# A Golay-code filter and a two-expert layer on one core: bits turned by one product for four tiles, router pairs in four operations

## The chip, the cores and the metric

The kernel runs on one core of a Trainium2 chip. The metric is device time in microseconds (us), the median of several runs; lower is better. A further execution was recorded by the hardware profiler; its own time and span are given below. PE is TensorE, DVE is VectorE, ACT is ScalarE, POOL is GpSimd and SP is SyncE.

## The reference, cut to what matters

The input has 16384 tokens of 512 numbers. Each token is normalized, filtered along its 512 numbers by a circulant filter whose constants depend on the data, and projected to 24 bits. The bits are corrected by a code of 12 checks. The normalized token also goes to two of eight experts.

```
xn   = layernorm(x)                                # 16384 x 512
x1   = real(ifft(fft(xn) * filt))
bits = (sigmoid(x1 @ W_el + b_el) > 0.5)           # 24 per token
syn  = (bits @ H.T > 0.5)                          # 12 checks
w    = syn.sum(-1)
bits = where(0 < w <= 3, (bits + first three of syn) mod 2, bits)
s    = x1 + bits @ W_le + b_le
p    = softmax(xn @ router_w.T)                    # 8 experts
v, i = top_k(p, 2);  c = v / (v.sum + 1e-6)
g    = silu(sum over both of (xn @ expert[i] + v) * c)
out  = x + s * g
```

As w is at most 3 where a fix is made, the first three checks are all checks that failed, and the fix flips the bits 0 to 11 whose check failed.

## The kernel before, in words

Tokens lie in 128 tiles of 128 tokens, one token to a partition. Four tiles make a block (`TPT` = 4, one load of 1 MB), eight make a group (`GT` = 8), and sixteen a round (`RT` = 16). There are two passes, and in both the order of all instructions is written out by hand.

**The first pass** is `pass_1`, a loop over the tiles g. One turn of it issues, in this order: every fourth turn `take_ex` (L566, sums for a block its logits into `ex`), `fold` of tile g + 2, `level`, `total` and `spread` of tiles further ahead, `transpose` of tile g + 1 and `filt` of tile g. For one tile these are: `total` (DVE, L452: the two halves of a row added into pp, with the row's sum), `spread` (ACT, L472: a sum of squares), `fold` (DVE, L507 and L510, sums and differences of pp's halves; POOL, L512, the differences mm of the input's halves), `transpose` (PE, L519, four times; ACT, L521, copies pmt out), and `filt` (PE, L535, L536, L538; ACT, L541, writes yb). `store` (L551) sends a finished block of yb to the memory yd. `level` turns four row sums at a time into two numbers, by one ACT operation each: `low` (L465), minus four times the mean, which `fold` adds, and column 10 of the tile's record (L466), the mean, which the second pass reads.

After the tile's own work, one turn issues one operation of the list `now` and four of the list `routes`, and `throw(1)` issues one waiting scatter.

`now` holds, for each group, the five operations of `code`: `bits` (DVE, L577) compares 24 logits of eight tiles with a bound and writes them, 16 bits wide, into the record; `turn_bits(0)` and `turn_bits(4)` turn four tiles each so that the 24 bits lie on partitions (PE, L586, one product with the identity for each tile; ACT, L589, one copy of 24x512 out of PSUM); `syndrome` (PE, L596) multiplies the turned bits of each of the eight tiles by the 24x12 matrix `ht_b`; `correct` (DVE, L600 to L610) tests the checks and flips bits in the record.

`routes` holds, for each round, the operations of `route`, nearly all on DVE: a maximum and a softmax over eight logits, the two largest (`largest`, twice), `chosen` (L700, the sum of two one-hot rows, `sel`), `behind`, seven operations of `pair` (L726), `quads` (L740, sums over four tiles), an empty one, `rank` (PE, L748 to L772), `chances` (L665, L715 to L719: the two probabilities and the divisor), `weights` (L805 to L827: the two weights, the sum of the biases, and an exchange so that the smaller expert comes first), then `place` and `where` (positions in lists of the 28 pairs of experts), the sixteen scatters (POOL, L788, one indirect transfer each from `rec` to `lists`), `more` and an addition to `cum`, and `put_records` (SP, L627: the records go to yd in four transfers). `pair` for distance d multiplies `sel` of experts 0 to 7-d with that of experts d to 7; the 28 products of a token say which pair it chose.

The last group's `code` and the last round's `route` are issued in the second pass.

**The second pass** goes over tiles of one pair of experts each (`whole`, 28 at first and five later), over 61 tiles that straddle lists (`item`), and over a rest. For each tile POOL gathers the list's entry or addresses (`fetch_tok`), the tokens of x (xg, six tiles ahead) and of yd (yg, five ahead), all at L1154; `normalize` (DVE, L1208) subtracts the mean and multiplies; PE transposes (L1215) and multiplies by the experts (L1247); ACT and DVE combine (L1290 to L1298); `put` multiplies and adds (DVE, L1326) and sends the rows out (POOL, L1331), three tiles behind. In each turn it issues `throw(3)`, one operation of `now` and ten of `routes`, so the last round's operations are spread over the turns 0 to 5, and after them come operations that plan the later tiles (`whole_ops`, whose `kept` copies tokens, means and scales of the whole tiles).

Of the kernel before, what the change touches and what calls it, by code (L numbers as in the profile page):

```python
# [27 lines left out]
def pairs_of(ne=8):  # L28

    return [(a, a + d) for d in range(1, ne) for a in range(ne - d)]  # L30
# [3 lines left out]
def kernel(  # L34
# [114 lines left out]
    ht_b = p1c.tile([L, 12], BF16, name="ht_b")  # L149
# [39 lines left out]
    ht = sp.tile([L, 12], F32, name="ht")  # L189
# [253 lines left out]
    def total(g: int):  # L443

        k, j = groups[g // GT], g % GT
        if j == 0:
            k.sum = small.tile([P, GT], F32, name="sum")
            k.sq2 = small.tile([P, GT], F32, name="sq2")
            k.low = small.tile([P, GT], F32, name="low")
# [12 lines left out]
    def level():  # L462
        while means:
            k, js = means.pop()
            nc.scalar.activation(k.low[:, js], k.sum[:, js], AF.Copy, scale=-4.0 / E)  # L465
            nc.scalar.activation(k.rec[:, js, 10], k.sum[:, js], AF.Copy, scale=1.0 / E)  # L466
# [34 lines left out]
    def fold(g: int):  # L501
# [6 lines left out]
            sd[:, 0:Q], p[:, 0:Q], k.low[:, j : j + 1], p[:, Q:H], ALU.add, ALU.add  # L508
# [61 lines left out]
    def code(s: int):  # L570
# [3 lines left out]
        def bits():  # L574

            k.bits = bits_of(k.rec)[:, :, 0:L]
# [4 lines left out]
        def turn_bits(h):  # L581
            if h == 0:
                k.bt = small.tile([L, GT, P], BF16, name="bt", bufs=2)
            pg = ps_g.tile([P, 512], F32, name="pg")[0:L].rearrange("l (j t) -> l j t", t=P)
            for j in range(TPT):
                nc.tensor.matmul(  # L586
                    pg[:, j, :], k.bits[:, h + j, :], ident_b, start=True, stop=True
                )
            nc.scalar.copy(k.bt[:, h : h + TPT, :], pg)  # L589

        def syndrome():
            k.pg = ps_g.tile([P, 512], F32, name="pg")[:, 0 : GT * 12].rearrange(
                "p (j n) -> p j n", n=12
            )
            for j in range(GT):
                nc.tensor.matmul(k.pg[:, j, :], k.bt[:, j, :], ht_b, start=True, stop=True)  # L596

        def correct():
# [12 lines left out]
                k.bits[:, :, 0:12], k.bits[:, :, 0:12], fix, ALU.not_equal  # L611
# [20 lines left out]
    def route(n: int):  # L632
# [30 lines left out]
        def total():  # L663
            st.sm = new("sm", [P, S])
            v.tensor_reduce(st.sm, st.pb, AX.X, ALU.add)  # L665
# [32 lines left out]
        def chosen():  # L698
            st.sel = new("sel", SN, BF16)
            v.tensor_add(st.sel, st.hot1, st.hot2)  # L700
# [7 lines left out]
        def den_of():  # L708
            st.den = new("den", [P, S])
            v.tensor_add(st.den, st.sm, st.p2)  # L710

# [841 lines left out]
```

## Time and profile before

| | |
|---|---|
| median of 4 runs | 1467.51 us |
| lowest and highest run | 1463.81 and 1469.38 us |
| the profiled execution's own time | 1464.95 us |
| its span in the trace | 1463.2 us |
| mean TensorE clock granted in it | 0.969 of full |
| TensorE busy | 1338.8 us, 91% of the span |
| VectorE busy | 933.7 us, 64% |
| ScalarE busy | 603.7 us, 41% |
| GpSimd busy | 876.1 us, 60% |
| bytes moved by DMA | 234.27 MB |
| first pass, from the timeline | some 36 to 333 us |

Busy time counts the time in which an engine works on instructions; issuing of transfers and waiting for semaphores is not counted, and matmuls are pipelined with modelled ends. In a line of groups, `out<-in` are the names of the tiles, followed by partitions x elements and the count; then stand total busy time, the mean of one in ns, and the idle time just before them with what ended it.

### The profile page before, as it was taken

Reading aid. Unit: us, or ns where it says so; the run is one execution under the profiler, and the core shown is the slowest. Engines: PE = TensorE matmul, PEld = TensorE weight load, DVE = VectorE, ACT = ScalarE, POOL = GpSimd, SP = SyncE. Lnnn points to the kernel's source line nnn. Section 1 sums busy time; section 2 is a strip of 40 time slices with the busy share of each in tenths; the row PEclk is TensorE's granted clock in tenths of the full one; section 3 lists DMA queues with packets and bytes.
Section 4 is the critical chain, followed back from the end, with each engine's and each line's share of the span. In section 5 each row is a group of like instructions: output and inputs, shape, how many; then the busy total and the mean of one; then the engine's idle time right before and its main releaser. Section 6 shows DMA issues by size and latency. Waiting matters only on the chain.

```text
span 1463.2 us, 18162 instructions
## 1 busy us (share of the span) xinstructions
PE 1338.8 (91%) x4938; PEld 741.0 (51%) x4938; DVE 933.7 (64%) x2679; ACT 603.7 (41%) x1295; POOL 876.1 (60%) x855
## 2 busy tenths in 40 slices
PE   2999999997397999959999999999999999998996
PEld 2887777773143444424444444444444444444443
DVE  7798999972364588701111126768777787686784
ACT  4998999873221222202222222323333333232332
POOL 1357877676446454565555216777777777776741
PEclk9999999999698999989999999999999999999998
DMA  5799877735122332244444424555555555555531
GB/s 193 286 325 300 251 250 238 236 119 171 55 69 84 121 106 88 90 127 130 137 136 153 149 81 149 173 163 164 179 159 169 165 178 168 165 173 161 173 128 43
DMA packets 119215, 234.27 MB, mean 160 GB/s; under 512 B 37227, under 2 KB 70891, under 8 KB 115022
## 3 DMA queue, kind: packets, MB, share of 16 engines
q0 software_dynamic: 47264, 135.54, 30.5%
q1 hardware_dynamic: 70750, 96.81, 19.7%
q8 instruction: 43, 0.70, 0.2%
q10 hardware_dynamic: 1104, 0.78, 0.2%
q14 instruction: 54, 0.44, 0.1%
HBM read 145.31 MB, written 87.75 MB: 159 GB/s over the span
## 4 chain that ended last, share of the span: by engine, by line
PE 62%; issue 16%; POOL 10%; DVE 5%; ACT 3%; another core or an unknown queue 2%; DMA 2%; POOLq 0%; DVEq 0%; SPq 0%; ACTq 0%
PE pe L1247 40%; PE py L538 7%; PE pt L1215 4%; PE pt L519 3%; POOL out L1331 3%; POOL yg L1154 3%; POOL xg L1154 2%; PE py L535 2%; PE py L536 2%; POOL part L1154 1%; ACT no L472 1%; POOL entry L1154 1%; ACT yb L541 1%; PE pg L1280 1%
## 5 line engine op out<-in xcount | busy, mean ns | idle before, releaser
L1247 PE MATMUL pe<-w_sb,xt 128*128 x2104 | 949.1, 599 | 2.0 <-DVE acc L1297 1.5
L1247 PEld LDWEIGHTS pe<-w_sb,xt 128*128 128x128 f32 x2104 | 398.3, 192 | 425.0 <-issue 417.6
L1298 ACT ACTIVATE acc<-acc,yg 128x512 f32<-128x512 f32 x128 | 92.5, 722 | 420.4 <-DVE acc L1297 321.7
L1297 DVE SCALAR_TENSOR_TENSOR acc<-pe,yg,acc 128x512 f32<-128x512 f32 x101 | 75.7, 750 | 237.9 <-PE pe L1247 121.3
L1217 ACT COPY xt<-pt 128x512 f32<-128x512 f32 x162 | 93.9, 579 | 210.8 <-PE pt L1215 162.1
L1154 POOL DMA_INDIRECT yg<-yd,toks x101 | 111.4, 1103 | 114.8 <-ACT acc L1298 50.8
L1331 POOL DMA_INDIRECT out<-xg,toks x101 | 111.8, 1107 | 82.0 <-DVE xg L1326 55.5
L1208 DVE TENSOR_SCALAR xn<-xg,entry 128x512 f32<-128x512 f32 x61 | 33.6, 552 | 197.2 <-PE pt L1215 152.7
L512 POOL TENSOR_TENSOR mm<-xt 128x256 f32<-128x256 f32 x128 | 99.9, 781 | 97.3 <-PE pt L519 68.3
L788 POOL DMA_INDIRECT lists<-rec,dst x128 | 134.1, 1047 | 32.3 <-issue 22.1
L1215 PEld LDWEIGHTS pt<-ident,xn 128*128 128x128 f32 x648 | 81.5, 144 | 135.9 <-issue 93.7
L538 PE MATMUL py<-cm,pmt 128*128 128x288 f32 x512 | 147.0, 410 | 0.0
L1215 PE MATMUL pt<-ident,xn 128*128 128x128 f32 x648 | 100.7, 279 | 46.9 <-ACT xt L1217 24.3
L1294 ACT ACTIVATE acc<-pe,yg 128x512 f32<-128x512 f32 x101 | 68.9, 682 | 157.7 <-PE pe L1247 77.6
L1154 POOL DMA_INDIRECT xg<-in_x,toks x101 | 108.5, 1074 | 40.6 <-issue 28.4
L541 ACT ACTIVATE yb<-py,rec 128x640 f32<-128x640 f32 x128 | 101.6, 794 | 30.2 <-PE py L538 21.2
L1154 POOL DMA_INDIRECT xg<-in_x,entry x88 | 92.1, 1046 | 29.3 <-issue 26.5
L1154 POOL DMA_INDIRECT part<-ed,adr_r x54 | 63.3, 1172 | 65.0 <-DMA ed<-res 48.8
L1154 POOL DMA_INDIRECT entry<-lists,adr_i x61 | 63.1, 1035 | 64.2 <-DVE xn L1208 50.6
L538 PEld LDWEIGHTS py<-cm,pmt 128*128 128x128 f32 x512 | 91.6, 192 | 13.8
L1326 DVE TENSOR_TENSOR xg<-mix,xg 128x512 f32<-128x512 f32 x128 | 88.6, 692 | 5.6 <-issue 1.1
L472 ACT ACTIVATE no<-xt,sum 128x512 bf16<-128x512 f32 x128 | 91.0, 711 | 0.9 <-DVE pp L452 0.9
(270 smaller groups left out, 1762.1 us busy)
## 6 DMA issues: line engine op xcount, KB each, us to landing
xt<-in_x SPq DMA_DIRECT2D x32, 1024.0 KB
yd<-yb SPq DMA_DIRECT2D x32, 576.0 KB
yd<-yb SPq DMA_DIRECT2D x32, 512.0 KB
ed<-res SPq DMA_DIRECT2D x61, 256.0 KB
w_sb<-in_expert_w SPq DMA_DIRECT2D x8, 1024.0 KB
yd<-rec SPq DMA_DIRECT2D x36, 64.0 KB
lists<-rec,dst POOLq DMA_INDIRECT x128
xg<-in_x,toks POOLq DMA_INDIRECT x101
```

The lines of the kernel that those rows point to most:

```text
L472: nc.scalar.activation(no, xts[g // TPT][:, g % TPT, :], AF.Square, bias=k.sum[:, j : j + 1], scale=-float(E), accum_out=k.sq2[:, j : j + 1],)
L512: nc.gpsimd.tensor_tensor(m, xr[:, 0:H], xr[:, H:E], ALU.subtract)
L538: nc.tensor.matmul(py[:, 1, 0 : X + H], pmt[:, 2 + c, :], cm[:, c, :], start=(c == 0), stop=(c == 1))
L541: nc.scalar.activation(y_room(g), py[:, :, 0:WY], AF.Copy, scale=k.rec[:, j, 11:12])
L788: dma = nc.gpsimd.indirect_dma_start(out=lists, out_offset=bass.IndirectOffsetOnAxis(ap=st.dst[:, j : j + 1], axis=0), in_=st.rec.bitcast( ...
L1154: nc.gpsimd.indirect_dma_start(out=dst, out_offset=None, in_=src, in_offset=bass.IndirectOffsetOnAxis(ap=idx, axis=0), bounds_check=limit - 1,
L1215: nc.tensor.transpose(pt[:, c * P : (c + 1) * P], k.xn[:, c * P : (c + 1) * P], ident)
L1217: nc.scalar.copy(k.xt.rearrange("p c t -> p (c t)"), pt)
L1247: nc.tensor.matmul(pe.unsqueeze(1), k.xt[:, c, :], w_sb[:, bass.ds(e, 1), c, :], start=(c == 0), stop=(c == KC - 1),)
L1298: nc.scalar.activation(k.acc, k.acc, AF.Silu, bias=k.rec[:, 9:10])
L1326: nc.vector.tensor_add(k.x, k.mix, k.x)
L1331: dma = nc.gpsimd.indirect_dma_start(out=of, out_offset=bass.IndirectOffsetOnAxis(ap=k.tok, axis=0), in_=k.x, in_offset=None, bounds_check ...
```

## The change

In the first pass the bits get a tile of their own, and the four tiles of a block are turned by one product with the identity, 96 columns to 96 partitions. `ht_b` becomes a matrix of 96x48 with the code's matrix four times on its diagonal, so that one product checks four tiles. The corrected bits 0 to 11 are written to the record by `correct`, the others by a new copy on GpSimd in `syndrome`. `level` keeps one operation of its two: column 10 of the record now holds minus four times the mean, `fold` reads it there, and in the second pass `kept` (for whole tiles) and `normalize` (for item tiles) multiply it by -0.25.

The pairs are taken around a circle: for distances 1, 2 and 3 all eight experts a with a + d modulo 8, for distance 4 only four. For that `sel` is twelve wide, its first four columns copied behind, and `pairs_of` gives the pairs in the new order. `quads` adds in two steps instead of reducing. The two probabilities lie side by side in one tile `ch` and the two weights in `wt`, so that `weigh` and `biases` are one operation each instead of two, and the sum with 1e-6 is one operation. The list of `route` is four operations shorter: three pairs and `den_of`.

```diff
-    return [(a, a + d) for d in range(1, ne) for a in range(ne - d)]
+    near = [(a, (a + d) % ne) for d in range(1, ne // 2) for a in range(ne)]
+    return [tuple(sorted(k)) for k in near] + [(a, a + ne // 2) for a in range(ne // 2)]
...
     bel_r = row_sb[:, 3 * NPAIR :]
-    ht_b = p1c.tile([L, 12], BF16, name="ht_b")
+    ht_b = p1c.tile([TPT * L, TPT * 12], BF16, name="ht_b")
...
     lat = sp.tile([P, KC, X], F32, name="lat")
-    ht = sp.tile([L, 12], F32, name="ht")
+    ht = sp.tile([TPT * L, TPT * 12], F32, name="ht")
     scales = (2, 4, 8, 16, 32)
...
             k.sq2 = small.tile([P, GT], F32, name="sq2")
-            k.low = small.tile([P, GT], F32, name="low")
         xr = xts[g // TPT][:, g % TPT, :]
...
             k, js = means.pop()
-            nc.scalar.activation(k.low[:, js], k.sum[:, js], AF.Copy, scale=-4.0 / E)
-            nc.scalar.activation(k.rec[:, js, 10], k.sum[:, js], AF.Copy, scale=1.0 / E)
+            nc.scalar.activation(k.rec[:, js, 10], k.sum[:, js], AF.Copy, scale=-4.0 / E)
...
         nc.vector.scalar_tensor_tensor(
-            sd[:, 0:Q], p[:, 0:Q], k.low[:, j : j + 1], p[:, Q:H], ALU.add, ALU.add
+            sd[:, 0:Q], p[:, 0:Q], k.rec[:, j, 10:11], p[:, Q:H], ALU.add, ALU.add
         )
...
-            k.bits = bits_of(k.rec)[:, :, 0:L]
+            k.bits = small.tile([P, GT, L], BF16, name="bits", bufs=2)
             nc.vector.tensor_tensor(
...
         def turn_bits(h):
             if h == 0:
-                k.bt = small.tile([L, GT, P], BF16, name="bt", bufs=2)
-            pg = ps_g.tile([P, 512], F32, name="pg")[0:L].rearrange("l (j t) -> l j t", t=P)
-            for j in range(TPT):
+                k.bt = small.tile([TPT * L, GT // TPT, P], BF16, name="bt", bufs=2)
+            pg = ps_g.tile([P, 512], F32, name="pg")[0 : TPT * L, 0:P]
+            nc.tensor.matmul(
+                pg, k.bits[:, h : h + TPT, :].rearrange("p j l -> p (j l)"), ident_b, start=True, stop=True
+            )
+            nc.scalar.copy(k.bt[:, h // TPT, :], pg)
+        def syndrome():
+            pg = ps_g.tile([P, 512], F32, name="pg")[:, 0 : GT * 12]
+            k.pg = pg.rearrange("p (j n) -> p j n", n=12)
+            nc.gpsimd.tensor_copy(bits_of(k.rec)[:, :, 12:L], k.bits[:, :, 12:L])
+            for h in range(GT // TPT):
                 nc.tensor.matmul(
-                    pg[:, j, :], k.bits[:, h + j, :], ident_b, start=True, stop=True
+                    pg[:, h * TPT * 12 : (h + 1) * TPT * 12], k.bt[:, h, :], ht_b,
+                    start=True, stop=True,
                 )
-            nc.scalar.copy(k.bt[:, h : h + TPT, :], pg)
-        def syndrome():
-            k.pg = ps_g.tile([P, 512], F32, name="pg")[:, 0 : GT * 12].rearrange(
-                "p (j n) -> p j n", n=12
-            )
-            for j in range(GT):
-                nc.tensor.matmul(k.pg[:, j, :], k.bt[:, j, :], ht_b, start=True, stop=True)
...
             nc.vector.tensor_tensor(
-                k.bits[:, :, 0:12], k.bits[:, :, 0:12], fix, ALU.not_equal
+                bits_of(k.rec)[:, :, 0:12], k.bits[:, :, 0:12], fix, ALU.not_equal
             )
...
             st.sm = new("sm", [P, S])
+            st.den = new("den", [P, S])
+            st.ch = small.tile([P, 2, S], F32, name="ch", bufs=1)
+            st.wt = small.tile([P, 2, S], F32, name="wt2", bufs=1)
             v.tensor_reduce(st.sm, st.pb, AX.X, ALU.add)
...
         def chosen():
-            st.sel = new("sel", SN, BF16)
-            v.tensor_add(st.sel, st.hot1, st.hot2)
+            st.sel = new("sel", [P, S, NE + NE // 2], BF16)
+            v.tensor_add(st.sel[:, :, 0:NE], st.hot1, st.hot2)
+            v.tensor_copy(st.sel[:, :, NE:], st.sel[:, :, 0 : NE // 2])
...
-        def den_of():
-            st.den = new("den", [P, S])
-            v.tensor_add(st.den, st.sm, st.p2)
         ops += [chosen, behind]
...
             total,
-            lambda: v.reciprocal(st.sm, st.sm),
-            lambda: v.tensor_mul(st.p2, st.p2, st.sm),
-            den_of,
-            lambda: v.tensor_scalar(st.den, st.den, 1e-6, None, ALU.add),
+            lambda: v.reciprocal(st.ch[:, 0, :], st.sm),
+            lambda: v.tensor_mul(st.ch[:, 1, :], st.p2, st.ch[:, 0, :]),
+            lambda: v.scalar_tensor_tensor(
+                st.den, st.ch[:, 0, :], 1e-6, st.ch[:, 1, :], ALU.add, ALU.add
+            ),
             lambda: v.reciprocal(st.den, st.den),
...
                 st.oh = new("oh", [P, S, NPAIR], BF16)
+            n = min(NE, NPAIR - at)
             v.tensor_mul(
-                st.oh[:, :, at : at + NE - d], st.sel[:, :, 0 : NE - d], st.sel[:, :, d:NE]
-            )
-        at = 0
-        for d in range(1, NE):
-            ops.append(lambda d=d, at=at: pair(d, at))
-            at += NE - d
+                st.oh[:, :, at : at + n], st.sel[:, :, 0:n], st.sel[:, :, d : d + n]
+            )
+        for d in range(1, NE // 2 + 1):
+            ops.append(lambda d=d: pair(d, (d - 1) * NE))
...
             st.q4 = small.tile([P, 4, NPAIR], BF16, name="q4", bufs=1)[:, 0:A]
-            with nc.allow_low_precision("counts up to 4"):
-                v.tensor_reduce(
-                    st.q4, st.oh.rearrange("p (a b) k -> p a k b", b=4), AX.X, ALU.add
-                )
+            o4 = st.oh.rearrange("p (a b) k -> p a b k", b=4)
+            two = small.tile([P, 4, 2, NPAIR], BF16, name="q2", bufs=1)[:, 0:A]
+            v.tensor_add(two, o4[:, :, 0:2, :], o4[:, :, 2:4, :])
+            v.tensor_add(st.q4, two[:, :, 0, :], two[:, :, 1, :])
...
         def weigh():
-            st.w1 = new("w1", [P, S])
-            v.tensor_mul(st.w1, st.sm, st.den)
-            st.w2 = new("w2", [P, S])
-            v.tensor_mul(st.w2, st.p2, st.den)
+            v.tensor_mul(st.wt, st.ch, st.den.unsqueeze(1).to_broadcast([P, 2, S]))
...
-            v.tensor_mul(st.sm, st.sm, st.w1)
-            v.tensor_mul(st.p2, st.p2, st.w2)
+            v.tensor_mul(st.ch, st.ch, st.wt)
...
             v.tensor_tensor(st.lo, st.athot1, st.athot2, ALU.is_gt)
-            v.tensor_sub(st.den, st.w1, st.w2)
+            v.tensor_sub(st.den, st.wt[:, 0, :], st.wt[:, 1, :])
...
             biases,
-            lambda: v.tensor_add(st.rec[:, :, 9], st.sm, st.p2),
+            lambda: v.tensor_add(st.rec[:, :, 9], st.ch[:, 0, :], st.ch[:, 1, :]),
             swap,
             lambda: v.tensor_mul(st.lo, st.lo, st.den),
-            lambda: v.tensor_add(st.rec[:, :, 0], st.w2, st.lo),
-            lambda: v.tensor_sub(st.rec[:, :, 1], st.w1, st.lo),
+            lambda: v.tensor_add(st.rec[:, :, 0], st.wt[:, 1, :], st.lo),
+            lambda: v.tensor_sub(st.rec[:, :, 1], st.wt[:, 0, :], st.lo),
         ]
...
             nc.vector.tensor_copy(toks[part], k.pt[:, 2, :])
-            nc.vector.tensor_copy(stats[part], k.pt[:, 0:2, :])
+            nc.vector.tensor_scalar(
+                stats[part][:, 0, :], k.pt[:, 0, :], -0.25, None, ALU.mult
+            )
+            nc.vector.tensor_copy(stats[part][:, 1, :], k.pt[:, 1, :])
             ready.add(("whole", part))
...
         k.tok = entry[:, 2:3]
-        k.mean, k.scale = (entry.bitcast(F32)[:, i : i + 1] for i in range(2))
+        k.low, k.scale = (entry.bitcast(F32)[:, i : i + 1] for i in range(2))
...
         k.xn = w1.tile([P, E], F32, name="xn2")
+        if k.kind == "item":
+            k.mean = w2.tile([P, 1], F32, name="mean1", bufs=2)
+            nc.vector.tensor_scalar(k.mean, k.low, -0.25, None, ALU.mult)
         nc.vector.tensor_scalar(k.xn, k.x, k.mean, k.scale, ALU.subtract, ALU.mult)
...
+    golay_4 = np.zeros((96, 48), np.float32)
+    for j in range(4):
+        golay_4[24 * j : 24 * j + 24, 12 * j : 12 * j + 12] = golay_t
...
         "basis": basis,
-        "golay_t": golay_t,
+        "golay_t": golay_4,
         "square": square,
```

## The prediction

> **What bounds the kernel now.** I read the page first (busy shares, slices, the chain that ended last), then the busy times in chosen stretches, then the groups of pass 1 with shapes kept apart, the chain of waits inside one round, and the timeline of VectorE, GpSimd and SyncE where the change touches them. A difference under 0.3% (4.4 us) is what a measurement of this kernel can't tell from none.
>
> From the page, busy times and the head of the chain that ended last:
>
> ```profile
> PE 1338.8 (91%) x4938; PEld 741.0 (51%) x4938; DVE 933.7 (64%) x2679; ACT 603.7 (41%) x1295; POOL 876.1 (60%) x855
> ...
> PE 62%; issue 16%; POOL 10%; DVE 5%; ACT 3%; another core or an unknown queue 2%; DMA 2%; POOLq 0%; DVEq 0%; SPq 0%; ACTq 0%
> ```
>
> TensorE seems to bound everything. By stages it is different:
>
> ```profile
> core 0: us, PE busy (x) PEld busy (x) DVE busy (x) ACT busy (x) POOL busy (x), PEclk, DMA share, GB/s
> 73.00:110.00 37.00, 36.98 (x240) 29.68 (x240) 34.89 (x131) 35.74 (x87) 19.57 (x23) 1.00 1.01 325
> ...
> 163.97:200.81 36.84, 36.12 (x234) 28.79 (x233) 35.85 (x129) 34.98 (x85) 29.08 (x32) 1.00 0.80 244
> ...
> 622.00:900.00 278.00, 260.50 (x786) 127.42 (x785) 49.06 (x105) 70.39 (x133) 130.06 (x129) 0.97 0.42 132
> ```
>
> The second line is one round of pass 1 (16 tiles, 36.84 us from one rank block to the next): PE idles 0.7 us, DVE 1.0, ACT 1.9. Three engines are full at once, so pass 1 shortens only by what the least relieved of them gains. In 73 to 110 us the DMA share is 1.0 as well. In the item stage (last line) PE sets the pace and DVE is 18% busy.
>
> One round's chain of waits (start, us, what) shows the same, passing from ACT to DVE to PE:
>
> ```profile
> 181.45 0.80 ACT yb L541
> 182.28 0.60 DVE ex L566
> ...
> 196.62 0.47 DVE oh L726 x4
> 197.09 0.35 issue
> 197.45 0.66 PE pt L519 x4
> ```
>
> DVE carries it from 182.3 to 197.1, ending on the pairs that the change edits; PE then has it to about 214.
>
> **What the change costs, part by part, for a round.** The groups (busy, mean ns | idle before) that give the prices, over seven or eight rounds:
>
> ```profile
> L586 PE MATMUL pg<-ident_b,rec 128*24 128x128 bf16 x124 | 12.2, 221 | 0.4 <-DVE pl L779 0.4
> L596 PE MATMUL pg<-ht_b,bt 24*128 24x12 bf16 x120 | 5.3, 165 | 0.0
> L589 ACT CAST bt<-pg 24x512 bf16<-24x512 f32 x31 | 17.3, 559 | 2.7 <-PE pc L1268 2.7
> L465 ACT ACTIVATE low<-sum 128x4 f32<-128x4 f32 x29 | 5.7, 198 | 0.0
> L740 DVE TENSOR_REDUCE q<-oh 128x112 bf16<-128x448 bf16 x7 | 6.5, 925 | 0.2
> L718 DVE TENSOR_SCALAR den<-den 128x16 f32<-128x16 f32 x7 | 2.8, 400 | 0.2
> ```
>
> PE: turning the bits takes 4 matmuls per block now, 1 then. A mean of 221 ns overlaps its neighbours; in the stream four follow each other at 0.08 us, so three saved are 0.24 us, times 4 blocks 0.97. The syndrome goes from 8 to 2 matmuls twice a round; they follow at 0.035 us, so 6 x 0.035 x 2 = 0.42 at most, and 0.24 if the wider ones (96 rows, 48 columns) take double. PE is relieved by 1.2 to 1.4, say 1.3.
>
> ACT: the copy 24x512 becomes 96x128. The nearest row is the cast of ct<-pc, 96x128, at 262 ns: 559 - 262 = 0.30, times 4 is 1.2. One of two row means goes: 0.2 x 4 = 0.8 by duration, 0.1 each by start-to-start, so 0.4 to 0.8. ACT is relieved by 1.6 to 2.0.
>
> DVE: the seven pair products stand 0.92 us from first to end. Four instead, three of 128 elements and one of 64, with the first at 0.14 start-to-start and the last not overlapped at 0.25, take 0.55, and the new copy of 64 elements 0.1: 0.26 saved (bounds 0.1 and 0.4). The reduce of quads, 925 ns, becomes two adds of 224 and 112 elements; between the 112-element product at 248 ns and the 128-element f32 sum at 348 ns, with overlap, 0.45 for both: 0.48 saved (bounds 0.25 and 0.6). The dropped op on den is 0.2 start-to-start undisturbed, 0.4 by its mean row. Weigh and biases lose one short op each, 0.09 apart: 0.18. Together 1.1, bounds 0.75 and 1.6.
>
> Against DVE stands GpSimd. The timeline:
>
> ```profile
> 198.03 0.93 DVE L740 TENSOR_REDUCE q<-oh 128x112 bf16<-128x448 bf16 x1
> 203.51 0.74 POOL L512 TENSOR_TENSOR mm<-xt 128x256 f32<-128x256 f32 x1
> 203.58 0.82 DVE L510 TENSOR_TENSOR sd<-pp 128x128 f32<-128x128 f32 x1
> ```
>
> L510 takes 0.28 alone and 0.82 beside mm, 0.54 lost; the reduce at 198.03 ran beside another mm (198.27 to 198.99) at its usual length. So the two adds enter a competition from which the reduce was free. mm runs 0.74 of a 2.3 us tile, a third of the time: two adds each lose 0.27 on average in a third of cases, 0.18 a round. The new GpSimd copy (12 of 24 bits of 8 tiles, twice a round) is not in the trace; between nothing, if no two-input op meets it, and mm's whole 0.74 each, I take 0.1 each, as it has 96 elements a row against mm's 256. It sits on GpSimd's queue ahead of a scatter and an mm; GpSimd has 7.8 us free a round, which covers it. DVE's net gain is 1.1 - 0.18 - 0.2 = 0.7, bounds 1.6 and -0.9.
>
> The Trainium skill, SBUF — State Buffer, section Who interferes with whom, says that a VectorE instruction with two SBUF inputs and a GpSimd instruction that reads SBUF lock each other out whole, and that a reduce never does. The rows above agree with both halves. By the rule at its worst, with both adds always locked out, the quads' whole gain would be lost, and the change as a whole would bring about 3 us less than the sum below.
>
> The round: PE 1.3, ACT 1.6, DVE 0.7. The chain changes hands inside a round, so it gains between DVE's 0.7 and PE's 1.3; I take 0.9, bounds -0.9 (DVE at its lower end) and 1.4. Seven rounds make 6.3, group 0 before them 0.65 (PE). Until about 120 us this is partly lost: the yb buffer waits for its store (2.78 us of ACT waiting for DMA yd<-yb at 120.45, handed on to PE as 2.52 at 122.76), with loads, stores and experts filling the queues. I take off 1.5. Pass 1: -5.5.
>
> Second pass. The last group's code runs there: PE -0.7, hidden by gathers, taken at 0.3. The route lists are four operations shorter and popped four a tile, so pass 1 throws one scatter more and GpSimd finds one fewer (a scatter stands 1.3 us from the next): up to 1.3, taken at 0.5. The new scaling of the gathered mean, a 128x1 DVE op on 61 item tiles, costs nothing beside 229 idle us of 278 in that stage; without cover it would be 61 x 0.17 = 10. The two ops of kept cost under 0.5. The row mean's scale of -4 and reading it from rec change no duration.
>
> In the second pass ten operations are popped per tile, and four fewer end the list one tile sooner: the store of the last round's records is issued a tile before it was. It still needs the corrected bits, so its data does not come sooner:
>
> ```profile
> 399.46 1.02 POOL L1154 DMA_INDIRECT yg<-yd,toks  x1 [14.90 <-ACT ct L1272]
> 415.25 2.56 SPq L627 DMA_DIRECT2D yd<-rec  x4
> 420.17 1.02 POOL L1154 DMA_INDIRECT yg<-yd,toks  x1 [15.28 <-DMA yd<-rec]
> ```
>
> Now the gather at 399.46 is ordered before that store; then it stands behind it and waits to about 419.5. Behind it on GpSimd's queue stand an out, a scatter and an xg (399.46 to 404.9, four issues at 1.33): 5.4 us of issues pushed past 420. The next x gather then starts near 436 instead of 430 for a use near 443, so I cost it at nothing, with 6 us of slack as cover. If that is gone, 5 to 11 us.
>
> Sum: -5.5 - 0.3 - 0.5 = -6. The profiled execution took 1464.95 us (span 1463.2 and 1.75 around it), which becomes 1459; it lies 2.6 below the median of 1467.51, so the median becomes 1461.5.
>
> **Rivals.** (a) DVE keeps pass 1: adds and copies are locked out by mm, and what is won before 120 us waits for yb's store. Gain 0.2 to 0.5 a round, 1.5 to 3.5 in all: 1464 to 1466. For it: DVE carries 15 us of the round's chain, and L825 (16 elements) took 0.81 beside mm. Against: not one of its edits adds elements.
>
> (b) All three are relieved by 1.3 or more, since the saved ops lie where DVE is late (196.62): 7.5 rounds of 1.3 to 1.5, less 1, with a shorter second pass: -9 to -12, 1456 to 1458.
>
> (c) Slower: the early store of records. Its place is GpSimd's queue at 399 to 420. PE stands still for 22.3 us at 365.8 and for 7.8 at 453, each while GpSimd issues indirect transfers without a break (343 to 384, 420 to 460). The pushed 5.4 us lengthen the second burst, x gathers come late, and the pause at 453 grows by 5.4 to 11. It decides once over 6 us are pushed; less a pass 1 gain of 0 to 4 it gives +5 to +8, 1472 to 1475.
>
> (d) The parts do not do what they say, as when the new reader and writer of rec add waits (fold now reads the mean there, while GpSimd and DVE write its bits): a semaphore wait of 0.2 on 8 tiles a round brings it to 0, 1467. It goes with (a).
>
> **How the numbers follow.** Forecast 0.40 (1459 to 1463), (b) 0.15, (a) with (d) 0.25, (c) 0.20. Faster is 0.40 + 0.15 = 0.55, same 0.25, slower 0.20. The range from 1455 to 1474 leaves out a part of (b) and of (c), about a tenth on either side; the likeliest case's own is 1459 to 1463.
>
> **What would show it.** Right: rank block to rank block near 36.0 us; the turn matmul once per block and its copy near 260 ns; DVE busy near 35 in a round; pairs and quads together near 1.1 us a round; the last scatter of pass 1 one tile earlier. (a) shows as the quads' adds over 0.6 and rounds of 36.5; (c) as a gather near 420 ahead of four issues, and a longer PE pause at 453. Wrong altogether: rounds as long as before with no engine within 2 us of full, or a change in the item stage's pace (3.87 us a tile).

## The result, and the profile after

The changed kernel is slower: median 1473.86 us against 1467.63 for the kernel before, ratio 1.0044 (95% interval 1.0029 to 1.0059). The forecast was 1461.5, faster. The profiled execution's span is 1466.6 us.

All numbers from the runs e, f, g, h and k below come from conditions in which TensorE was granted a clock of 0.98 to 0.99 and the kernel before takes 1378 to 1379 us; the result above and the runs m come from 0.97, where it takes 1456 to 1468. Each ratio is against the kernel before in the same conditions. The first pass ends 2 to 5 us earlier in the former than in the latter (333.0 and 337.65 before the change, 343.8 and 346.00 after).

From the page after, busy times:

```profile
PE 1332.8 (91%) x4746; PEld 738.3 (50%) x4746; DVE 947.4 (65%) x2710; ACT 591.5 (40%) x1263; POOL 874.9 (60%) x871
```

PE lost 192 instructions and 6 us, ACT 12 us. DVE, from which work was to be taken, has 14 us more. The busy times in stretches show where. The second line is a stretch as long as one round of sixteen tiles, which is 38.42 us now from rank block to rank block (161.18 to 199.60):

```profile
core 0: us, PE busy (x) PEld busy (x) DVE busy (x) ACT busy (x) POOL busy (x), PEclk, DMA share, GB/s
73.00:110.00 37.00, 35.10 (x214) 28.60 (x213) 35.60 (x120) 34.14 (x83) 22.18 (x27) 1.00 0.97 313
183.62:222.05 38.43, 35.26 (x211) 28.09 (x210) 37.46 (x124) 33.78 (x82) 30.09 (x35) 1.00 0.80 247
622.00:900.00 278.00, 261.58 (x792) 128.35 (x791) 54.06 (x159) 70.45 (x134) 130.02 (x130) 0.97 0.43 133
```

The round is 1.6 us longer than before (36.84). PE now idles 3.2 us of it and ACT 4.6; DVE idles 1.0, as it did. So the round is DVE's. The groups of pass 1, shapes kept apart, show that the edited operations do cost less and that others cost more (the first two lines are from before, the others from after):

```profile
L519 PE MATMUL pt<-ident,sd 128*128 128x128 f32 x250 | 50.9, 285 | 1.7 <-DVE oh L726 0.6 <-DVE sd L507 0.6 <-issue 0.3
L510 DVE TENSOR_TENSOR sd<-pp 128x128 f32<-128x128 f32 x124 | 42.3, 341 | 0.0
```

```profile
L585 PE MATMUL pg<-ident_b,bits 128*96 128x128 bf16 x31 | 6.8, 219 | 0.0
L518 PE MATMUL pt<-ident,sd 128*128 128x128 f32 x248 | 51.6, 285 | 12.4 <-DVE sd L506 8.7 <-DVE sd L509 2.7 <-DVE ex L565 0.5
L588 ACT CAST bt<-pg 96x128 bf16<-96x128 f32 x31 | 7.9, 254 | 0.0
L732 DVE TENSOR_TENSOR oh<-sel 128x128 bf16<-128x128 bf16 x24 | 7.4, 341 | 0.0
L745 DVE TENSOR_TENSOR q<-oh 128x224 bf16<-128x224 bf16 x8 | 2.2, 275 | 0.3
L746 DVE TENSOR_TENSOR q<-q 128x112 bf16<-128x112 bf16 x8 | 1.7, 217 | 0.3
L509 DVE TENSOR_TENSOR sd<-pp 128x128 f32<-128x128 f32 x123 | 51.6, 420 | 0.0
L593 POOL COPY rec<-bits 128x96 bf16<-128x96 bf16 x15 | 4.5, 300 | 0.1
```

The turning copy takes 254 ns instead of 559, the two additions 492 instead of 925. But the fold's subtraction L509, which the change does not touch (L510 before, 341 ns), takes 420 ns, 79 ns more in 123 tiles: 9.7 us. And PE's first transposes of a tile now wait 12.4 us, 11.4 of them for the fold; before, it was 1.7 in all.

The timeline shows one such stretch (start, length, engine, line; in brackets the idle time before):

```profile
210.05 0.62 DVE L788 TENSOR_REDUCE dst<-pl 128x16 int32<-128x448 f32 x1
211.43 1.17 POOL L792 DMA_INDIRECT lists<-rec,dst  x1 [2.45 <-ACT no L471]
212.61 0.80 POOL L511 TENSOR_TENSOR mm<-xt 128x256 f32<-128x256 f32 x1
212.01 0.82 DVE L509 TENSOR_TENSOR sd<-pp 128x128 f32<-128x128 f32 x1
212.75 0.94 DVE L452 SCALAR_TENSOR_TENSOR pp<-xt 128x256 f32<-128x256 f32 x1
```

The first scatter of a round stood 2.45 us; it reads the places that `where` (L788) writes until 210.67, and the releaser that the profile names, L471, does not write them. mm, behind that scatter on GpSimd's queue, falls on the subtraction and on the sum of the next tile: both are a good half microsecond longer than their usual length (0.28 and 0.41).

I call the time that DVE's operations take above their own usual length, where that is over 0.15 us, the collision loss (usual: the tenth part of executions that are shortest). Between the last yb of tile 64 and that of tile 80 it was 8.7 us before and 11.2 after, in 16 and 19 operations, and each of them lies over an mm. Measured by the end of the last yb, the first pass went from 337.65 to 346.00 us: 1.4 ahead at the first tile, 3.9 at tile 24, 0.7 behind at tile 40, 8.4 behind at the end.

Not all of it is collision loss: 3.2 us of the 8.4 come between the tiles 96 and 112, where that loss differs by 1.1 us (6.0 and 7.1). There GpSimd gathers from `lists` what the plan of the second pass needs (L912), once, at the end of a round's list. The next mm stands behind it, and PE's transposes of mm wait for that. Before, then after:

```profile
L912 POOL DMA_INDIRECT tt<-lists,idx x1 | 1.0, 987 | 3.2 <-PE pt L519 3.2
L519 PE MATMUL pt<-ident,mm 128*128 128x128 f32 x250 | 48.0, 274 | 2.2 <-POOL mm L512 2.2
```

```profile
L912 POOL DMA_INDIRECT tt<-lists,idx x1 | 1.0, 987 | 5.6 <-DMA lists<-rec,dst 5.6
L518 PE MATMUL pt<-ident,mm 128*128 128x128 f32 x248 | 47.5, 273 | 5.5 <-POOL mm L511 5.5
```

With the shorter list the gather stands one tile earlier on GpSimd's queue (109 of the mm ahead of it, not 110). GpSimd stands 5.6 us ahead of it instead of 3.2, until scatters have landed as the profile names it, with the next mm behind; and PE waits 5.5 us for mm instead of 2.2. In no other tiles of the pass does PE wait for mm.

### The profile page after: what moved, and what is told of

Read it like the earlier page. It is cut to its first block, busy times and chain, and to the rows that moved or that the text cites. A ratio compares the mean times of both kernels' runs of the same rounds, so it can differ in the third digit from the quotient of the medians.

```text
span 1466.6 us, 17781 instructions
## 1 busy us (share of the span) xinstructions
PE 1332.8 (91%) x4746; PEld 738.3 (50%) x4746; DVE 947.4 (65%) x2710; ACT 591.5 (40%) x1263; POOL 874.9 (60%) x871
## 4 chain that ended last, share of the span: by engine, by line
PE 40%; issue 19%; POOL 14%; DVE 12%; another core or an unknown queue 6%; DMA 4%; ACT 3%; POOLq 1%; SPq 1%; DVEq 0%; ACTq 0%
PE pe L1253 30%; POOL xg L1157 3%; POOL yg L1157 3%; POOL out L1337 3%; PE pt L1221 3%; PE py L537 3%; POOL part L1157 2%; DVE pp L452 2%; DVE sd L506 1%; DMA lists<-rec,dst 1%; DVE sd L509 1%; PE pt L518 1%; DMA yd<-yb 1%; POOL entry L1157 1%
## 5 line engine op out<-in xcount | busy, mean ns | idle before, releaser
L1214 DVE TENSOR_SCALAR xn<-xg,mean,entry 128x512 f32<-128x512 f32 x61 | 34.2, 561 | 193.1 <-PE pt L1221 148.5
L471 ACT ACTIVATE no<-xt,sum 128x512 bf16<-128x512 f32 x128 | 91.5, 715 | 5.0 <-DVE pp L452 4.8
```

What stands on the lines that cost most here:

```text
L471: nc.scalar.activation(no, xts[g // TPT][:, g % TPT, :], AF.Square, bias=k.sum[:, j : j + 1], scale=-float(E), accum_out=k.sq2[:, j : j + 1],)
```

## The experiments

The table has one row for each kernel: its ratio with the interval, the end of the first pass, the stretch from tile 64 to 80 and the collision loss in it. The last three rows are in the other conditions.

| kernel | ratio to before | first pass ends | tiles 64 to 80 | loss |
|---|---|---|---|---|
| before (f1) | 0.9996 [0.9982, 1.0010] | 333.0 | 36.88 | 8.7 |
| change (f2) | 1.0083 [1.0066, 1.0100] | 343.8 | 38.43 | 11.2 |
| before, mm cut (f3) | 0.9969 [0.9950, 0.9987] | 332.5 | 36.03 | 0.4 |
| change, mm cut (f4) | 0.9962 [0.9947, 0.9976] | 325.7 | 33.86 | 0.2 |
| change, padded lists (e1) | 1.0006 [0.9995, 1.0017] | 336.9 | 36.98 | 10.0 |
| bits alone (e3) | 0.9986 [0.9977, 0.9995] | 335.0 | 37.81 | 9.8 |
| router alone (e4) | 1.0040 [1.0026, 1.0054] | 338.5 | 37.66 | 10.5 |
| mean alone (e5) | 1.0005 [0.9996, 1.0014] | 336.3 | 37.57 | 9.8 |
| change, mm in halves | 1.0131 [1.0113, 1.0148] | 347.1 | 39.25 | 12.0 |
| before, mm in halves | 1.0010 [1.0000, 1.0019] | 337.1 | 38.03 | 10.2 |
| change, three buffers | 1.0063 [1.0047, 1.0078] | 343.3 | 39.39 | 12.2 |
| before, one empty operation | 0.9982 [0.9973, 0.9992] | 331.3 | 36.03 | 6.7 |
| change, lists a turn later | 1.0065 [1.0047, 1.0083] | 338.7 | 37.84 | 10.6 |
| bits alone, copy on ACT | 0.9978 [0.9969, 0.9987] | 331.7 | 36.92 | 9.7 |
| padded, copy on ACT | 0.9999 [0.9988, 1.0009] | 334.3 | 36.80 | 9.8 |
| bits, ACT, one empty | 0.9965 [0.9932, 0.9998] | 338.7 | 38.06 | 10.4 |
| padded, ACT, one empty | 0.9992 [0.9954, 1.0029] | 336.5 | 36.98 | 10.1 |
| bits, ACT, two empty | 0.9998 [0.9964, 1.0032] | 341.0 | 38.16 | 10.4 |

**The parts.** Three theories stood at the start: O, the shorter list's order; P, the collisions; S, the early store of records in the second pass. The list was padded, and each part was put alone into the kernel before.

```diff
 # e1: the change, with the places of den_of and of three pairs kept
             lambda: v.tensor_mul(st.ch[:, 1, :], st.p2, st.ch[:, 0, :]),
+            *([lambda: None] if True else []),
...
             ops.append(lambda d=d: pair(d, (d - 1) * NE))
+        if True:
+            ops += [lambda: None] * 3
```

> The change whole, with three empty operations put into each round's list where three pairs went and one where the sum with the divisor went, so that every other operation is issued in the same turn as before the change. Theory O (order): the change loses time because rank, place, where and the scatters moved one turn earlier, onto turns in which VectorE is already full; then the first pass ends (last yb) near 332 us against 337.65 before and 346.00 after, and the total is near 1461. Theory P (port): the loss is in additions and subtractions of the fold that meet GpSimd's mm by the phase that they happen to have; then the padded order gives another phase, the sums of the fold still lose 2 us a round or more against their shortest length, the first pass ends at 338 to 346 and the total is 1468 to 1474. Theory S (second pass, the early store of the records): the first pass is as after the change, and 3 to 6 us come back behind it.

> The kernel before with the bits' part alone: one turning product for four tiles, block-diagonal checks, the copy of twelve bits on GpSimd. Lists are as long as before. Theory O: PE and ACT are relieved, VectorE and the order are untouched, so the first pass ends 0 to 5 us earlier than 337.65 and the total is 1462 to 1467. Theory P: the faster turns of PE move mm against the fold; with VectorE full the first pass ends 3 to 8 us later and the total is 1470 to 1475.

> The kernel before with the router's part alone: pairs around a circle, quads by two additions, chances and weights side by side, lists four operations shorter. Theory O: this holds the whole loss, the first pass ends 5 to 9 us later than 337.65 and the total is near 1474. Theory P: fewer operations on VectorE, phase unknown: the first pass ends between 332 and 342 and the total is 1461 to 1472. If the two additions of quads are locked out by mm they take over 0.6 us a round together.

> The kernel before with the row mean's part alone: one ScalarE operation for four tiles instead of two, the fold reads the record, means scaled by -0.25 in the second pass. Theories O and P: 0.1 to 0.2 us of ACT for four tiles, VectorE untouched; the first pass ends within 2 us of 337.65 and the total within 3 us of before. A third theory R (the fold has to wait for other writers of the record) would show as waits of the fold on GpSimd or ACT, 0.2 us a tile, and a first pass longer by 5 us or more.

The loss sits in the router's part, +0.40%. The bits' part alone is faster by 0.14%, though its first pass ends 2.0 us later than f1's: its gain comes behind it (155.1 us from there to the 17th finished tile of the second pass, 158.8 in f1). The mean's part is worth nothing that can be told. With padded lists the whole change is where the kernel before is: its order, more than its operations, costs the time. But O's number for the padded kernel, 332 us and 1461 (6 us below before), is missed too: all the relief is there, and little of it shows (the tiles 48 to 64 take 35.06 us instead of 36.03, the tiles 64 to 80 no less than before). In this round every one of the four has a higher loss than the kernel before, even the mean's, which only takes an ACT operation away. A single round says little of a single part, however: over the whole pass the loss is 54.0 us with the mean's part, 60.1 to 63.2 with the other three, 67.7 and 69.8 in two executions of the change, and 54.8 and 58.7 in two of the kernel before.

**The collisions taken out.** GpSimd's mm was cut to 16 of 256 columns, in both kernels; the rest of the tile stays at zero, so half of the filter's input is missing.

```diff
-        m = front.tile([P, H], F32, name="mm")
-        nc.gpsimd.tensor_tensor(m, xr[:, 0:H], xr[:, H:E], ALU.subtract)
+        m = mms[g % 2]                   # two tiles, set to zero once
+        nc.gpsimd.tensor_tensor(m[:, 0:16], xr[:, 0:16], xr[:, H : H + 16], ALU.subtract)
```

> The kernel before, unchanged, to have its profile on the same chip as the next three. All theories: the first pass ends (last yb) at 337 to 339 us, as in the profile shown, since the two profiles agree there if nothing but the second pass differs between executions.

> The changed kernel, unchanged, on the same chip. If the parts measured alone add up (bits -1.9 us, router +5.5, mean +1.0) it is 4 to 6 us slower than before. Theory O (order) and theory P (port): the first pass ends 5 to 9 us later than in the kernel before. Theory S (second pass): 3 us or more of the loss lie between the last yb and the 17th finished tile of the second pass.

> The kernel before with GpSimd's difference mm cut from 256 to 16 columns (the other columns stay at zero), so that it can hardly meet the fold's sums; this leaves out half of the filter's input. Theory P: the fold's sums lose under 1 us a round against their shortest length instead of 4.6, and the first pass ends 5 to 12 us earlier than with the full mm. Theory O: nothing of the order changes, so the first pass ends within 3 us of the full kernel's.

> The changed kernel with the same cut of mm to 16 columns. Theory P: with no collisions left, the change shows the gain that was forecast: its first pass ends 4 to 10 us earlier than that of the kernel before with mm cut. Theory O: the turns that the shorter list overfills stay overfull, and its first pass ends 2 to 8 us later than that of the kernel before with mm cut.

The expectation for f1 was 4 us off: the first pass ended at 333.0, not 337 to 339. Of the 4.7 us to the profile shown, 1.5 are there at the first tile and 3.2 come in the last sixteen. The round from tile 64 agrees to 0.04 us, and its loss too (8.7 in both), so it is the better measure; the one behind it does not (37.80 and 38.28 us, with losses of 6.9 and 8.9).

For the fold's operations over 183 to 260 us, groups by form: before, after, before with mm cut, and the change with mm cut:

```profile
L510 DVE TENSOR_TENSOR sd<-pp 128x128 f32<-128x128 f32 x32 | 11.1, 348 | 0.0
```

```profile
L509 DVE TENSOR_TENSOR sd<-pp 128x128 f32<-128x128 f32 x31 | 16.0, 516 | 0.0
```

```profile
L512 DVE TENSOR_TENSOR sd<-pp 128x128 f32<-128x128 f32 x34 | 9.9, 291 | 0.0
```

```profile
L511 DVE TENSOR_TENSOR sd<-pp 128x128 f32<-128x128 f32 x36 | 10.5, 292 | 0.0
```

The subtraction costs 291 or 292 ns without mm, 348 with it before, 516 after: 0.17 us in each of 16 tiles, 2.7 us a round more. Without mm the change does what was forecast and more: the round falls from 36.03 to 33.86, by 2.17 us, and the first pass ends 6.8 us earlier. With mm it ends 10.85 later. So mm at its full width takes 17.7 us from the change's lead.

Two things are in this. From tile 16 to 96 PE waits for no mm in any of the four kernels; there the change loses 5.0 us with mm, where its collision loss is 50.7 us against 40.1, and gains 2.6 without. Between tile 96 and 112 the change loses 5.4 us more with mm, though its collision loss is the lower there (5.9 us against 7.8): this goes with the gather of the plan, behind which PE waits 6.3 us for mm in the changed kernel and not at all in f1. With mm cut the wait is 6.2 us against 3.1, so it grows there without collisions too. In the six profiles of the shorter list started in the old turn (after, f2, f4, e4, halves, three buffers) GpSimd stands 5.3 to 8.0 us ahead of this gather; in the other fourteen, the padded and the later lists among them, 2.7 to 4.2. No run changes this gather's place alone, and PE's wait does not follow it closely (4.5 us in e1).

Busy time from 183 to 220 us, the kernel before with mm cut, then the change with mm cut:

```profile
183.00:220.00 37.00, 36.98 (x239) 29.71 (x240) 29.57 (x133) 35.74 (x86) 20.23 (x34) 1.00 0.85 250
```

```profile
183.00:220.00 37.00, 37.00 (x230) 30.94 (x229) 30.09 (x137) 35.95 (x89) 23.25 (x37) 1.00 0.90 278
```

Both are bound by PE, with 7 us of DVE free; so PE's relief shows there. By tile, four turns and two syndromes are shorter: in the steps of tiles 75 to 77, from 2.43, 2.52 and 2.30 us to 2.03, 2.12 and 2.06.

Of the 6.8 us only 3.0 reach the 17th finished tile of the second pass, and in the total the two kernels with mm cut are not told apart (1374.13 and 1373.71). The profile of the change with mm cut shows where a part of the 3.8 us went. The records' store and the gather behind it (SP, POOL):

```profile
372.26 8.70 SPq L631 DMA_DIRECT2D yd<-rec  x4
383.32 1.02 POOL L1161 DMA_INDIRECT yg<-yd,toks  x1 [7.04 <-DVE mix L1299]
```

and the same in the kernel before with mm cut:

```profile
386.85 2.65 SPq L629 DMA_DIRECT2D yd<-rec  x4
392.53 1.02 POOL L1158 DMA_INDIRECT yg<-yd,toks  x1 [4.45 <-DMA yd<-rec]
```

The store is issued earlier, its four parts are drawn out over 8.7 us, and the gather behind them waits 7.0 us where the other waits 4.5; 1.0 us of the lead is lost from the first finished tile to the 17th. The profile names an operation on DVE, not the store, as what released that gather, so that the store costs this is not shown. The other 2.8 are lost before the first finished tile. In f2 and f1 the stretch from the last yb to the 17th tile is 158.9 and 158.8 us, so S plays no part in the change's loss in these conditions. From the 17th tile to the last it is 875.4 to 876.1 in all fifteen kernels of these conditions.

**Attempts to make collisions cheaper.** First, mm in two halves; then more buffers for sd and mm.

```diff
-        nc.gpsimd.tensor_tensor(m, xr[:, 0:H], xr[:, H:E], ALU.subtract)
+        for a in range(0, H, H // 2):
+            b = a + H // 2
+            nc.gpsimd.tensor_tensor(m[:, a:b], xr[:, a:b], xr[:, H + a : H + b], ALU.subtract)
```

> The changed kernel with GpSimd's difference mm issued as two instructions of 128 columns in place of one of 256; nothing else differs and nothing is left out. From the rows of mm at 16 columns (0.24 us) and 256 (0.72) a half takes some 0.46, so GpSimd has 0.2 us a tile more to do. Theory P (port): a VectorE operation that is locked out now waits for a half only, so VectorE's loss of 11.2 us a round falls to some 6, rounds shorten from 38.4 to 34.5 to 36.5, the first pass ends 6 to 14 us earlier than 343.84 and the total is 1376 to 1384. Against it (GpSimd full, or shorter gaps that collide as often): rounds stay at 38 or more and the total at 1390 or more.

> The kernel before with the same split of mm. It is bound by PE within 0.7 us a round, so theory P gives rounds of 36.0 to 36.5 instead of 36.9 (as with mm cut to 16 columns, 36.03), a first pass that ends 0 to 4 us earlier and a total of 1374 to 1379: much less than the changed kernel gains from the split. If the changed kernel with the split comes out faster than this one, the change's own relief is shown with all of its output computed.

> The changed kernel with three buffers instead of two for sd and for mm. With two, both the fold's sums and mm start when PE's transposes release the buffers of the tile two before, so that they tend to start together. Theory P, with the phase set by this common release: mm starts earlier, when GpSimd is free, the collisions change (VectorE's loss 6 to 10 us a round instead of 11.2), and the first pass ends 2 to 10 us earlier than 343.84. If the phase is set by VectorE's own lag, nothing moves by more than 2 us.

All three missed. A half is shorter (505 ns), but the DVE operations that lost over 0.15 us in the round rose from 19 to 32: each half can meet another one (28 of the 32 lie over an mm, four over a scatter alone), and the loss is 12.0 us, not 6. The kernel before lost by the split as well: its round is 38.03 us instead of 36.88, with a ratio of 1.0010 and an interval from 1.0000. More buffers moved the loss up to 12.2, and the end of the first pass by 0.6 us, within the 2 us that stood for a phase set by VectorE's own lag. Making mm start at another moment did not take the competition away.

**What sets the phase.** Phase means here where DVE's operations fall against the starts of mm. One empty operation at the head of each list, with no instruction added; the lists started a turn later; the new copy on ACT.

```diff
 # k_before_noop, on the kernel before
-        ops = [begin, shift]
+        ops = [lambda: None, begin, shift]
 # k_after_later, on the change
-                if g == t + size + 1:
+                if g == t + size + 2:
 # k_bits_act on e3, k_pad_act on e1
-            nc.gpsimd.tensor_copy(bits_of(k.rec)[:, :, 12:L], k.bits[:, :, 12:L])
+            nc.scalar.copy(bits_of(k.rec)[:, :, 12:L], k.bits[:, :, 12:L])
```

> The kernel before with one empty operation at the head of each round's list: no instruction is added or removed, and the operations of the list up to the pairs stand one place later in the order on VectorE. Theory P with a phase: VectorE's collision loss in the round from tile 64 to 80 (8.7 us) and the round (36.88 us) change by 0.5 us or more, in most cases upward since the kernel before lies low, and the first pass ends 1 us or more from 333 to 337. If the phase does not matter, round and loss stay within 0.2 us.

> The changed kernel with each round's list started one turn later in the first pass, so that rank, place and where are issued in the turns of the kernel before, and the first half of the list one turn later than there; the work is the changed kernel's. Theory O (rank and place must lie on the turns of before): as with the padded list, rounds near 37 and a first pass that ends near 337. Theory P with a phase that any shift resets: collision loss between 9 and 12 us a round, rounds of 37 to 39, first pass 337 to 346.

> The bits' part alone, with the copy of twelve bits on ScalarE instead of GpSimd: a version to beat the kernel before. The GpSimd copy reads memory and can lock VectorE out twice a round; ScalarE has 1.2 us a round to spare from the shorter copies. If the copy's collisions cost anything, VectorE's loss (9.8 us in the round from tile 64) falls by 0.3 to 0.6 us, and the total is 0.1 to 0.3% below before; if not, it is as the bits' part alone, 0.14% below.

> The whole change with padded lists and the copy of twelve bits on ScalarE. If the GpSimd copy is what moves the phase, collision loss in the round from tile 64 falls from 10.0 us to 8.7 or less and the total is 1 to 5 us below before; if the phase is set by PE's shorter turns and the list, it stays at 1379 to 1382.

The empty operation shows that order alone moves the loss: the same instructions, the list's operations one place later, and the loss falls from 8.7 to 6.7 us, the round to 36.03, the length that PE sets (as with mm cut). In the round ahead the loss falls as much (8.5 to 6.7), but that one took 36.03 us already: a loss costs time only where it makes DVE later than PE. Busy time from 183 to 220 us, the kernel before and the same with the empty operation:

```profile
183.00:220.00 37.00, 36.22 (x235) 28.89 (x234) 36.01 (x129) 35.13 (x87) 29.25 (x33) 1.00 0.80 246
```

```profile
183.00:220.00 37.00, 36.98 (x242) 29.69 (x241) 34.99 (x132) 35.75 (x87) 29.88 (x34) 1.00 0.84 255
```

DVE's busy time falls by a microsecond, and PE is full. I had expected a change upward. The later start puts rank and place on the turns of before, but the round stays at 37.84 with a loss of 10.6: theory O in its strict form, that those turns are what matters, falls. The copy on ACT takes 0.2 us of loss from this round (9.8 to 9.7), where 0.3 to 0.6 were expected, and 1.7 from the one ahead of it (8.3 to 6.6). The version has the lowest median so far with all its output computed, 0.22% below the kernel before, though it can't be told from the empty operation's 0.18%. In the padded change it moves the ratio from 1.0006 to 0.9999, less than can be told, and the loss only from 10.0 to 9.8, not to the 8.7 that would have made the GpSimd copy the cause.

**Relief and phase together.**

> A version to beat both: the bits' part with its copy on ScalarE, and one empty operation at the head of each round's list, which alone brought the kernel before 2.5 us. If relief and phase add up: rounds from tile 64 of 34.5 to 36, collision loss under 9 us, first pass ends near 329, total 1372 to 1374. If the phase is set anew by each change of pace, the empty operation gives nothing predictable: 1373 to 1380.

> The whole change with padded lists, the copy on ScalarE and one empty operation at the head of each round's list. If relief and phase add up: first pass near 331, total 1375 to 1377. If not: 1376 to 1383, with a collision loss of 9 to 11 us in the round from tile 64.

> As the first, with two empty operations at the head. With two, the list before the pause ends still in its sixth turn, so rank and place keep their turns, and only the order of single operations against mm moves. If loss is set by phase alone, rounds and loss differ from those with one empty operation by 0.5 us or more in either direction; if one place was what mattered, the two are within 0.3 us.

They do not add up. The empty operation that took 2 us of loss from the kernel before gives 10.4 in the bits' version, against 9.7 without; a second one gives 10.4 as well. The phase seems to be set anew by each change of pace. One of the three lies below before, 0.9965 with an interval that ends at 0.9998. Of the versions that take work away, the bits alone with the copy on ACT lies clearest below the kernel before, at a clock of 0.99; at 0.97 it was not run.

## Why the prediction was wrong

Its steps, one by one. **PE's relief** was mis-sized: 1.3 us a round forecast, 2.1 in the steps of tiles with mm cut; a turn of four tiles saves 0.40 us, not the 0.24 taken from starts 0.08 apart (in the trace before they lie 0.06 apart, which would give 0.17; what saves the rest is not shown). **ACT's** price for the copy was right (0.30 each), but its busy time in the round fell by 1.2 us (34.98 to 33.78), not by 1.6 to 2.0. **DVE's own operations** came out near the forecast of 1.1: the additions 0.49 together against 0.45, the four pair operations and the copy at most 1.4 by summed lengths that overlap, and DVE's busy time less the collision loss falls from 27.2 to 26.3 us a round, by 0.9. **The item stage** pays nothing for its new operation, as said. **The early store** cost nothing that shows in f2; with mm cut, where the first pass ended early, some 1 us of the lead was lost in the stretch where rival (c) placed it. The store was not tried alone. **The stretch up to 130 us** swallowed more than the 1.5 us taken off: a lead of 3.9 us at tile 24 was gone at tile 40.

The step that failed is the term of the competition between DVE and GpSimd. It was costed for the new operations alone, 0.18 us for the additions and 0.2 for the copy, and the collisions that were already there were left out of the sum as if they were constant. They are 8.7 us of DVE's round, and DVE had 1.0 us to spare. They rose by 2.5 us, which is more than the 0.9 won, and as DVE bounds the round the sum turns over: +1.6 instead of -0.9.

A second term was left at nothing. The sum priced the shorter list as one scatter more thrown in pass 1, a gain of 0.5 us, and looked for its harm in the second pass alone. It left out that the plan's gather in pass 1 stands at the end of such a list: issued a tile earlier it comes with 3.2 of the 8.4 us that the first pass lost in the result's profile, and 5.4 of 10.85 in f2.

Rival (a) had the place (DVE keeps pass 1 because of mm) but not the size, nor the sign: it looked for the loss in the new additions, which stayed cheap (0.49 us), and what was put against it, "not one of its edits adds elements", says nothing of operations that no edit touches. Rival (c) named the time by luck: 1473.86 lies in its 1472 to 1475, but the loss is not where it put it. From the last yb to the 17th finished tile, the changed kernel takes as long as the kernel before in f2 and f1, and 7.5 us less in the result's profile (186.9 against 194.4). The mechanism is in the round's timeline that the prediction showed (L510 beside mm), and in its groups: L510 took 341 ns on average where half of its executions take 281 or less. Times sixteen, with the same for L507 and the sums, a large part of that loss stood there to be read.

The Trainium skill, SBUF — State Buffer, section SBUF: two separate sides, says that whichever of the two engines starts first has the shared ports for its whole instruction, and that the other waits. In the stretch at 212 us the sum agrees: it starts within mm (212.61 to 213.41) and ends 0.28 us after it. The subtraction agrees less well: at its usual length it would have ended at 212.29, before mm begins in the profile, and it ended at 212.83, within mm; what held it is not shown. The halves agree: a lock for a whole instruction is not made cheaper by two instructions that are each met.

What stays open: at a clock of 0.99 the loss of the first pass stays to the end (10.85 us at its end, 10.95 at the 17th tile, 10.3 at the last). In the conditions of the result the second pass holds further pauses, and the profiled executions differ by 8.35 us at the end of the first pass, 0.9 at the 17th tile and 3.4 at the last; so that the first pass causes the median's 6.2 us there is argued from the other conditions, and not shown. Nor is it shown which single operation's place fixes the phase; only that every shift moved it. And no order was found that holds the change's whole relief, 2.2 us a round, with mm at its full width.

## What to carry to other kernels

Where two engines lock each other out and one of them is full, the lockout is a term of the sum of its own: add up, over a round, what operations take above their shortest length, and ask how it moves, before counting what an edit saves. In a kernel whose three engines are all within 2 us of full, the order decides which operations happen to meet. An edit that takes work away changes that too, and so it can lose; try the same edit with the old places kept, and try shifts that change no work. Look as well for the one gather or store at the end of a list: a shorter list issues it earlier, and what stands behind it waits. To learn what an edit is worth in itself, take the competitor out in both kernels and compare those, stage by stage.

## What the hardware showed that was not expected

One empty entry in a list, without any change in the instructions, took 1.8 and 2.0 us of collision loss out of the two rounds from tile 48 to 80; the second of them became 0.85 us shorter, the first, which PE sets, no shorter, and the whole 0.18% faster (0.9982, interval 0.9973 to 0.9992). mm took 0.24 us for 16 columns, 0.5 for 128 and 0.77 for 256, so that splitting it costs GpSimd 0.2 us a tile, and the operations that lost over 0.15 us rose from 19 to 32.
